# Two graph layers in fp32: half-width sums that share PSUM banks, mixes in a row, a reworked last pair and a new plan

## The chip, the cores and the metric

One core of a Trainium2 chip runs the kernel. The metric is the device time of one execution in microseconds; times are medians of the runs.

## What is computed

The input is x, 128 batches of 128 nodes with 512 features, and an adjacency matrix of 128 x 128 integers for each batch, all in fp32 or int32. Two layers follow each other, cut to what matters:

```python
# layer 0: attention with 8 heads of 64
q, k, v = (x @ W + b for W, b in ((Wq, bq), (Wk, bk), (Wv, bv)))
attn = softmax(where(adj > 0, q @ k.T / 8, -1e9))        # per head
x = layernorm(x + relu((attn @ v) @ Wo + bo))
# layer 1: graph attention
Wh = x @ W
e = leaky_relu((Wh @ a1)[:, None] + (Wh @ a2)[None, :], 0.2)
att = softmax(where(adj == 0, -1e9, e))
x = layernorm(x + elu(att @ Wh))
```

## The kernel before

Two batches are a pair, and there are 64 pairs. The two batches' rows make a matrix of 256 x 512 whose product with a weight of 512 x 512 is done in blocks in Strassen's manner: seven products of half size (PRODUCTS, L414) are summed in three PSUM banks, A (products 0 and 2), B (1, 3, 5) and C (4, 6). DVE and ScalarE add and subtract what the banks hold at fixed points in the row. The sums of blocks that the products take as operands are made on GpSimd, which the profile calls POOL (left_sums, L422; results sx, so, sz).

Per pair the steps are:
- q and k together: full-width products (columns_product, L528; banks of 128 x 512, 8 matmuls of 128 x 128 each). q^T and k^T come out, with biases added on ScalarE (with_bias, L614).
- v, o and w: half-width products (rows_product, L519; 2 matmuls of 128 x 256 each). Reading the banks takes half_p1, half_p6, half_c11, half_p7, half_c22, half_c21 and half_c12 (L709 to L774), which leave e1a, e1b, u2, u3 and the four blocks of the result (cv, co, cw).
- logits (L776): 8 matmuls per batch that use half of the rows of TensorE, into the pool ps_att. Masking, maximum, exponential, sum and scaling follow on DVE and ScalarE (L794 to L816).
- The weights of the softmax are transposed: by blocks of 32 on DVE, then through DRAM with a DMA out and four in (weights_t, weights_out, weights_in, L818 to L849). The last pair uses TensorE (ppT).
- mix_values (L851): 8 matmuls per batch that use half of the columns of TensorE, into po. mix_values_out (L860) adds bv on ScalarE and makes o^T (oT), the operand of the o products.
- residual, layer norm (L556 to L573; the steps rstd and shift on GpSimd), and the two edge sums per node on DVE (edge_term, L881).
- The edges of layer 1 (L891 to L960): the sums e_j are brought from a column into a row by a 32-wise transpose on DVE (ej) and four DMAs (ejr), e is summed on ScalarE, made leaky, masked and searched for its maximum on DVE, and raised on ScalarE (at). at is transposed by DVE and DMAs through DRAM (atb, atd, attT), but in the last pair on TensorE (pat, copied by ScalarE).
- mix_nodes (L962): 4 matmuls per batch into pz, copied to zT by ScalarE (L969), then the w products, elu (exponential on ScalarE, L991, the cut at one on GpSimd, L996, the maximum on DVE, L1000), residual and layer norm, and the store.

In the last pair side_engine (L418) puts GpSimd's sums and residuals on DVE, and the o and w products are plain ones with rows of the weights loaded again (plain_product, L690).

PSUM has these users: ps_att with two buffers of two banks (tag att), ps_acc with one bank for each of accA, accB and accC, and ps with one bank (tag ps), which po, pz, pat and the prologue's transposes share. With one buffer, the next user of a tag waits until the last reader of the one before is done.

The order of the work is written by hand. Each step is an event with a time of its own, and every engine, SyncE's DMA queue among them, takes its instructions in that order:

```python
shift = ENDS.get(p if p < n_pair // 2 else p - n_pair, {}).get(key, 0.0)
events.append((p * PERIOD + PLAN[key] + shift, len(events), fn, args))
```

The times are in the plan's own unit; only their order counts. A pair takes 36.74 us in the trace, between the starts of two logits. ENDS moves the steps of the first and last pairs, GOING (L284) puts unneeded matmuls (keep_going) behind some of them, and BUFS (L286) says how many buffers each SBUF tile has. The weights and biases are loaded by the lines L448 to L469: Wq, Wk and the first x on the queues of SyncE and ScalarE, Wv, Wo, W and a on SyncE's, the biases on GpSimd's.

Of the kernel before, what the change touches and what calls it, by code (L numbers as in the profile page):

```python
# [8 lines left out]
F32 = mybir.dt.float32  # L9
I32 = mybir.dt.int32  # L10
AF = mybir.ActivationFunctionType
# [6 lines left out]
PERIOD = 78.768558  # L18
PLAN = dict(
    load_adj=-214.2762, load_blocks=-156.4567, x_transpose0=-118.9579, sums_qk=-118.4185, sums_v=-116.8612,  # L20
    sums_fold1=-64.8766, x_transpose1=-64.055, sums_fold0=-58.8898, sums_fold_t1=-54.4418, qk0=-36.0224,
    x_sums=-35.8404, sums_fold_out1=-33.087, qk1=-32.9779, qk_p1=-31.7105, fill_logits0=-31.5232, qk4=-28.6459,
    qk_p6=-28.5331, sums_fold_t0=-28.2956, qk_p1q=-27.7049, qk2=-26.3155, qk_c11=-24.8916, sums_fold_out0=-23.0845,
    qk3=-22.6254, v0=-21.402, qk_p7=-19.9439, qk_c22=-19.9339, qk5=-14.7467, qk6=-13.4439, sums_o=-9.6234,
    qk_c21=-7.8856, qk_c12=-7.8498, v_p1=-4.7268, v1=-4.5449, fill_logits1=-1.8505, mask=-1.2435, v_p6=-0.2943,
    logits=0.0, mask_logits0=1.9952, max_logits0=3.7429, v3=4.4065, v_p7=4.433, v2=7.4467, v_c11=9.2069, v4=9.2085,
    mask_logits1=10.0374, load_x1=10.3213, v5=13.2871, v_c22=14.6665, exp_logits0=14.7511, v_c21=15.0921,
    v6=17.2266, v_c12=17.5754, max_logits1=22.1216, sum_logits0=24.0633, norm_logits0=27.409, exp_logits1=33.3029,
    weights_t0=43.7048, sum_logits1=43.7767, norm_logits1=52.0118, weights_out0=53.6197, weights_t1=55.6065,
    sums_w=66.7876, weights_out1=68.011, weights_in0=70.4393, weights_in1=74.301, mix_values0=75.8522,  # L30
    mix_values_out0=80.7212, mix_values1=81.4334, mix_values_out1=85.4398, load_x0=87.1711, o_sums=101.6394,
    o0=106.2181, o_p1=113.6365, o1=113.6652, o4=115.875, o_p6=116.2192, o_p1l=117.1503, o3=117.1603, o_p7=117.3205,
    o2=117.7709, o_c11=118.2449, o_c22=118.2872, o5=120.8539, o6=121.6955, o_c21=121.8792, residual01=122.7569,
    o_c12=122.7614, stats01=122.8191, mean01=123.8502, residual00=127.7304, rstd01=128.2803, shift01=128.7729,
    stats00=130.3078, norm01=131.2371, mean00=131.4538, rstd00=133.9815, edge_term01=134.3884, shift00=135.5918,
    edge_term11=137.3863, norm00=140.4496, edge_term10=144.2793, edge_blocks=146.1519, fill_edges=152.9599,
    edge_row=155.4786, edge_term00=159.9559, edge_sums=163.3873, edge_leaky=169.0665, edge_mask=174.9959,
    edge_max=179.2956, edge_exp=184.846, edges_t=185.9311, edges_t_out=188.282, edges_t_in=189.7663,
    mix_nodes1=211.95, mix_nodes_out1=218.2462, mix_nodes0=220.5122, mix_nodes_out0=222.7905, z_sums=231.0565,
    w0=248.2279, edge_norm=250.3865, w_p1=253.8429, w1=254.0225, w2=254.7456, w_p6=256.7486, w3=258.7144,  # L40
    w_c11=259.1252, w4=262.9461, w_p7=264.5461, w5=268.1992, w_c22=268.2862, w6=268.4953, w_c21=269.0061,
    w_c12=270.9016, elu_exp1=288.3615, elu_exp0=298.9658, elu_low1=307.1177, elu_max1=314.1197, elu_low0=326.1878,
    elu_max0=338.6625, residual10=340.2052, stats10=349.6362, mean10=349.9591, residual11=350.8328, rstd10=358.934,
    stats11=386.2458, mean11=395.8811, shift10=413.3316, rstd11=414.603, shift11=416.7025, finish0=436.5642,
    finish1=440.8676, store0=451.5942, store1=492.1186, tail_exp=492.2186, tail_max=492.3186, tail_sum=492.4186,
    tail_norm=492.5186)
# [3 lines left out]
        qk_p1=-683.1417, qk_p1q=-681.9305, x_transpose0=-638.4435, x_transpose1=-631.2847, qk_p6=-590.8687,  # L50
        load_adj=-509.98, qk0=-477.8452, qk1=-452.442, qk2=-417.202, qk_c11=-405.3261, load_blocks=-378.6558,
        qk_c21=-372.1296, load_x1=-349.2729, mask=-346.6978, fill_logits0=-342.4208, qk3=-323.1482,
        tail_max=-298.4256, qk_p7=-287.7433, load_x0=-275.5939, x_sums=-254.831, qk_c12=-246.448, logits=-211.8037,
        qk_c22=-200.6414, qk5=-195.7663, fill_edges=-195.5757, fill_logits1=-146.0062, mask_logits0=-117.0145,
        norm_logits0=-112.6679, v2=-110.5345, sum_logits0=-110.267, weights_t0=-109.2774, max_logits0=-108.9309,
        v_p1=-107.9734, mask_logits1=-107.2963, exp_logits0=-105.8888, sum_logits1=-105.473, exp_logits1=-105.4285,
        v4=-104.5453, v6=-103.1904, v3=-103.169, v_c22=-102.5766, v1=-102.4315, v_p6=-101.2639, v_c11=-99.6798,
        v5=-98.0298, weights_in0=-97.1349, weights_out0=-96.6864, norm_logits1=-96.608, weights_t1=-95.7185,
        max_logits1=-95.6542, v_p7=-94.2704, v0=-92.9615, v_c12=-91.0601, o_sums=-86.6133, v_c21=-85.4889,
        o0=-84.7601, o1=-84.5751, mix_values0=-83.3707, o_p6=-81.6679, o_p1=-81.5774, o4=-79.0618, o3=-76.7214,  # L60
        o_p1l=-75.7272, mix_values_out1=-73.9311, mix_values_out0=-73.1278, o_p7=-70.8784, mix_values1=-70.4988,
        edge_norm=-69.258, weights_in1=-63.5621, o2=-61.8681, o5=-61.4743, o_c11=-59.3031, weights_out1=-59.1716,
        qk6=-53.9952, o_c22=-52.8877, residual01=-49.6326, o6=-49.6072, o_c21=-49.0819, residual00=-47.774,
        o_c12=-45.863, rstd01=-45.0658, residual11=-44.5158, store1=-42.4846, mean01=-42.4551, stats01=-42.0697,
        stats11=-41.2343, shift01=-37.2547, edge_term00=-30.8626, stats00=-30.155, mean00=-28.7366, rstd00=-27.6003,
        edge_term10=-26.5946, norm00=-25.0273, elu_exp0=-23.9225, shift00=-21.9905, norm01=-20.8832,
        elu_low0=-20.7084, mean11=-19.7227, w4=-16.199, edge_term01=-15.574, elu_low1=-15.5655,
        edge_blocks=-13.5721, elu_max1=-12.3739, edge_term11=-11.5908, rstd11=-10.9852, edge_max=-9.6908,
        edge_exp=-8.7377, elu_exp1=-8.6133, w1=-8.084, mix_nodes_out1=-7.3656, w_c22=-6.8246, w_p7=-5.7838,
        edge_mask=-5.5201, w5=-5.2206, w_p6=-4.9532, w_c12=-4.7308, w3=-4.5677, w_c21=-4.3597, edge_leaky=-4.2136,  # L70
        w_p1=-3.3698, finish1=-3.265, w6=-2.9974, mix_nodes1=-2.7204, w2=-2.7129, w0=-2.5504, elu_max0=-2.5273,
        w_c11=-1.1757, edges_t=-0.4981, edge_sums=-0.4753, mix_nodes0=3.5821, edge_row=5.2807, z_sums=7.0497,
        edges_t_out=7.4547, mix_nodes_out0=8.0879, shift11=9.5854, residual10=10.3581, edges_t_in=10.9727,
        finish0=20.2363, shift10=23.2537, stats10=23.7054, store0=34.1326, tail_sum=34.4037, mean10=40.9196,
        rstd10=58.9908, tail_norm=87.4954, qk4=98.1821, tail_exp=109.5699),
    1: dict(
        tail_norm=-486.5775, tail_max=-214.9271, fill_logits1=-130.5901, qk0=-114.6075, qk2=-113.2598,
        qk_p1q=-111.8967, qk1=-111.4589, qk_p6=-110.7816, qk3=-109.5867, qk_p1=-109.3704, x_sums=-109.3159,
        qk_p7=-108.414, tail_sum=-106.3184, qk4=-104.0469, qk_c11=-94.7644, x_transpose1=-89.4256, v3=-88.8756,
        v0=-88.5843, v_p6=-88.4612, qk5=-86.7206, load_x0=-86.6125, v_p1=-86.0976, qk_c21=-85.9776, v1=-85.847,  # L80
        qk_c12=-83.5311, qk6=-80.4324, max_logits1=-78.9744, v5=-78.6397, qk_c22=-76.8719, v_c21=-75.782,
        v_c11=-75.0503, sum_logits0=-74.7479, v_c22=-74.6319, v2=-74.4777, v4=-73.6934, mask=-72.5388,
        mask_logits1=-72.5341, mask_logits0=-70.3835, v_p7=-70.2904, max_logits0=-69.0883, logits=-68.7397,
        exp_logits0=-68.0694, v6=-67.8706, v_c12=-66.1552, weights_t0=-62.7498, fill_logits0=-61.6049,
        x_transpose0=-60.9054, exp_logits1=-56.6504, sum_logits1=-54.1366, weights_out0=-53.2933,
# [199 lines left out]

BUFS = dict(  # L286
    at=1, xb=2, adj=5, so=1, xT=3, sx=1, pr=2, qT=2, kT=2, scr=1, cw=6, e1a256=1, mask=2, u2256=1, u3256=1, cv=2,
    x=3, prb=1, e1a512=1, e1b512=1, u2512=1, u3512=1, prT=2, oT=2, e1b256=1, co=6, ejr=1, e=1, atb=1, attT=1, zT=2,
    sz=1, t=2)


# [845 lines left out]
```

## Time and profile before

| | us |
|---|---|
| median of 3 runs | 2398.43 |
| lowest, highest | 2397.58, 2399.31 |
| profiled execution, its time | 2399.47 |
| its span, first to last instruction | 2397.7 |
| busy: TensorE matmuls | 2374.3 |
| busy: DVE | 1865.7 |
| busy: ScalarE | 1555.9 |
| busy: GpSimd | 1409.3 |
| mean granted TensorE clock | 0.998 |

The span is that of one execution taken by the hardware profiler, and it is 1.8 us shorter than that execution's time. PE is TensorE's matmuls, PEld its weight loads, which run beside them, DVE VectorE, ACT ScalarE, POOL GpSimd and SP SyncE. A line such as L525 is the line of the kernel that issued the instruction. An fp32 matmul is two instructions in the trace. The ends of matmuls are modelled, so the distance between two starts says more than a length. A wait in brackets is idle time of the engine before the instruction and what ended it.

### The profile page before, as it was taken

The page shows a single profiled execution, that of the slowest core. Times are in us where ns is not written, and L with a number is a line of the kernel's source. Part 1 is how long each engine was busy: PE and PEld are TensorE (multiplying, and loading weights), DVE is VectorE, ACT ScalarE, POOL GpSimd, SP SyncE. Part 2 cuts the span into 40 slices and gives each one's busy share as a digit, 9 for nine tenths or more (in the row PEclk, how much of TensorE's full clock was granted, in tenths as well). Part 3 has the DMA queues.
Part 4 walks back from the last instruction along what each step waited for, and adds up shares of the span by engine and source line. Part 5 has one row for each costly group of instructions (what it writes and reads, how often), then busy time and mean ns, then how long its engine had stood idle before and what let it go on. Part 6 is the DMA issues. An engine that isn't in the chain of part 4 may idle for free.

```text
span 2397.7 us, 51833 instructions
## 1 busy us (share of the span) xinstructions
PE 2374.3 (99%) x17750; PEld 2146.1 (90%) x17750; DVE 1865.7 (78%) x3883; ACT 1555.9 (65%) x5512; POOL 1409.3 (59%) x1988
## 2 busy tenths in 40 slices
PE   8999999999999999999999999999999999999997
PEld 8999999989989989899899899998998998989985
DVE  6777787787777777877877778778777777777786
ACT  4666676666666766766666667666666676666664
POOL 3455665656565656556665655565656565656557
PEclk9999999999999999999999999999999999999999
DMA  7534434444445344444444443544544534444433
GB/s 189 125 92 108 120 106 124 118 112 123 115 103 134 101 116 123 105 124 116 102 134 108 111 125 101 124 117 112 122 114 105 134 100 118 121 107 122 102 93 84
DMA packets 341366, 276.59 MB, mean 115 GB/s; under 512 B 126384, under 2 KB 288944, under 8 KB 341104
## 3 DMA queue, kind: packets, MB, share of 16 engines
q1 hardware_dynamic: 339712, 271.70, 44.2%
q8 instruction: 142, 2.33, 0.4%
q10 hardware_dynamic: 1216, 1.31, 0.3%
q14 instruction: 120, 0.98, 0.2%
q0 software_dynamic: 176, 0.27, 0.1%
HBM read 156.90 MB, written 107.87 MB: 110 GB/s over the span
## 4 chain that ended last, share of the span: by engine, by line
PE 95%; DMA 1%; POOL 1%; ACT 1%; DVE 1%; issue 0%; SPq 0%; ACTq 0%; POOLq 0%; DVEq 0%
PE pBqk L536 14%; PE pCqk L536 9%; PE pAqk L536 9%; PE pBv L525 7%; PE pBw L525 7%; PE pBo L525 7%; PE po L857 5%; PE s L784 5%; PE pz L967 5%; PE pAv L525 5%; PE pCv L525 5%; PE pAo L525 4%; PE pCo L525 4%; PE pAw L525 4%; PE pCw L525 4%; DMA wqk<-in_L_gnn_Wq_dram 0%
## 5 line engine op out<-in xcount | busy, mean ns | idle before, releaser
L807 ACT ACTIVATE pr<-pr,nmax 128x128 f32<-128x128 f32 x1024 | 395.2, 389 | 0.5 <-DVE nmax L801 0.5
L816 ACT ACTIVATE pr<-pr,tot 128x128 f32<-128x128 f32 x1024 | 314.4, 411 | 43.7 <-DVE tot L811 43.6
L866 ACT ACTIVATE oT<-po,bv 128x128 f32<-128x128 f32 x512 | 144.7, 364 | 290.4 <-PE po L857 290.4
L1009 POOL TENSOR_TENSOR cw<-cw,co 128x512 f32<-128x512 f32 x126 | 158.6, 1278 | 214.8 <-DVE cw L1003 214.8
L563 POOL TENSOR_SCALAR rstd<-mv 128x1 f32<-128x1 f32 x255 | 95.2, 373 | 271.1 <-DVE mv L558 250.1
L998 POOL TENSOR_SCALAR t<-t 128x512 f32<-128x512 f32 x126 | 246.3, 1955 | 9.0 <-ACT t L994 8.6
L536 PE MATMUL pAqk<-xT,wqk 128*128 128x128 f32 x2016 | 245.7, 275 | 2.2 <-ACT e1bqk L616 2.2
L536 PE MATMUL pBqk<-sx,wqk 128*128 128x128 f32 x2016 | 245.6, 275 | 0.4 <-POOL rstd L563 0.4
L536 PE MATMUL pCqk<-sx,wqk 128*128 128x128 f32 x2016 | 245.7, 275 | 0.0
L536 PEld LDWEIGHTS pAqk<-xT,wqk 128*128 128x128 f32 x2016 | 236.4, 192 | 9.3 <-ACT e1bqk L616 2.4
L536 PEld LDWEIGHTS pBqk<-sx,wqk 128*128 128x128 f32 x2016 | 239.8, 192 | 3.8 <-POOL rstd L563 0.5
L536 PEld LDWEIGHTS pCqk<-sx,wqk 128*128 128x128 f32 x2016 | 235.5, 192 | 0.2
L792 POOL MEMSET pr<- 128x1024 f32 x128 | 121.8, 951 | 145.2 <-DVE prb L826 145.2
L888 DVE SCALAR_TENSOR_TENSOR scr<-co,wa_bc 128x512 f32<-128x512 f32 x256 | 185.4, 724 | 16.9 <-ACT co L573 11.6
L796 DVE COPY_PREDICATED pr<-mask,s 128x1024 f32<-128x1024 int32 x128 | 171.6, 1341 | 33.5 <-PE s L784 33.3
L807 ACT ACTIVATION_READ_ACCUMULATOR pr<-pr,nmax 128x1 f32 x1024 | 193.6, 189 | 0.0
L826 DVE STREAM_TRANSPOSE prb<-pr 128x1024 f32<-128x1024 f32 x126 | 156.1, 1239 | 17.6 <-ACT pr L816 16.5
L564 POOL TENSOR_TENSOR rstd<-rstd,half 128x1 f32<-128x1 f32 x255 | 145.5, 571 | 21.2
L801 DVE TENSOR_REDUCE nmax<-pr 128x8 f32<-128x1024 f32 x128 | 155.4, 1214 | 0.2
L857 PE MATMUL po<-prT,cv 128*64 128x128 f32 x2048 | 140.0, 279 | 0.1
L967 PE MATMUL pz<-attT,co 128*128 128x128 f32 x1024 | 136.8, 277 | 2.6 <-DMA attT<-atd 1.3
L525 PE MATMUL pBv<-wv,sx 128*128 128x256 f32 x512 | 137.4, 391 | 0.0
(197 smaller groups left out, 5920.0 us busy)
## 6 DMA issues: line engine op xcount, KB each, us to landing
prd<-prb SPq DMA_DIRECT2D x126, 512.0 KB, 2.9
prT<-prd SPq DMA_DIRECT2D x504, 128.0 KB, 3.6
x<-in_x_dram SPq DMA_DIRECT2D x128, 256.0 KB, 4.4
out_dram<-cw SPq DMA_DIRECT2D x128, 256.0 KB, 3.5
xb<-in_x_dram SPq DMA_DIRECT2D x252, 128.0 KB, 4.0
adj<-in_adj_dram SPq DMA_DIRECT2D x64, 128.0 KB, 2.1
ejr<-ej SPq DMA_DIRECT2D x256, 32.0 KB, 3.9
atd<-atb SPq DMA_DIRECT2D x63, 128.0 KB, 1.8
```

The lines of the kernel that those rows point to most:

```text
L525: nc.tensor.matmul(out, left_block(left, blk.pair, a_i, c), right_block(weight, b_i)[:, c, :], start=first and c == 0, stop=j in LAST and ...
L536: nc.tensor.matmul(out[:, f * P:(f + 1) * P], weight[:, b_i, c, f * P:(f + 1) * P], left_block(left, blk.pair, a_i, c), start=first and f ...
L796: nc.vector.copy_predicated(PR[b], MASK[p][:, i, :].unsqueeze(1).to_broadcast([P, H, P]), ST.pop(("s", b)).rearrange("p j h k -> p (j h) k"))
L801: nc.vector.tensor_reduce(NMAX[b], PR[b], AX.X, ALU.max, negate=True)
L807: nc.scalar.activation(PR[b][:, h, :], PR[b][:, h, :], AF.Exp, bias=nmax[:, h:h + 1], scale=1.0, accum_out=TOT[b][:, h:h + 1])
L816: nc.scalar.activation(PR[b][:, h, :], PR[b][:, h, :], AF.Copy, scale=tot[:, h:h + 1])
L826: nc.vector.transpose(PRB[b].rearrange("p k h s -> p h k s"), PR.pop(b).rearrange("p h (k r) -> p h k r", r=32))
L857: nc.tensor.matmul(ST["o", b][j * DH:(j + 1) * DH, hp, :], v[:, h * DH:(h + 1) * DH], prT[:, :, j * (H // 2) + hp, :], start=True, stop=True)
L888: nc.vector.scalar_tensor_tensor(scr, X1[b], 1.0, wa_bc[s], op0=ALU.mult, op1=ALU.mult, accum_out=acc)
L967: nc.tensor.matmul(ST["z", b][:, c, :], X1[b][:, c * P:(c + 1) * P], attT, start=True, stop=True)
L998: side_engine(b // 2).tensor_scalar(t, t, 1.0, -1.0, op0=ALU.min, op1=ALU.add)
L1009: side_engine(b // 2).tensor_tensor(Y[b], Y[b], X1.pop(b), op=ALU.add)
```

## The change

Six things are changed together:
- Blocks.psum: half-width sums A and C lie side by side in one bank, in accA for v and w and in accC for o. B stays in accB. Full-width sums keep three banks. In the last pair the plain o product A goes to accC.
- mix_values of the odd batch writes to accC instead of ps, so that the two mixes need not take turns. In the order, most pairs ran a mix, the logits of the next pair, and the other mix; now they run the logits and then both mixes.
- For the last pair: half of the scaling of the softmax goes to DVE, half of the reads of po and pz too, and the row of e_j is made by two DVE copies and two transposes on TensorE into PSUM, from where e is summed, in place of a DVE transpose and four DMAs.
- at is transposed on TensorE in the last two pairs, not in the last alone.
- bo is loaded by SyncE's queue behind a, not by GpSimd's.
- PERIOD, PLAN, ENDS, GOING and BUFS are new. In the first pair the plain q and k products run A, B, C, D, A, B, C, D instead of A, B, A, B, C, D, C, D.

The diff, with the tables PLAN and ENDS left out:

```diff
-PERIOD = 78.768558
+PERIOD = 81.828156
...
-GOING = {('w6', -3): 5, ('mix_nodes1', -2): 2, ('mix_nodes0', -2): 2, ('w2', -2): 2, ('w5', -2): 4, ('edges_t', -1): 1, ('mix_nodes1', -1): 2}
+GOING = {('edges_t', -2): 2, ('mix_nodes1', -2): 3, ('mix_nodes0', -2): 3, ('w0', -2): 2, ('edge_row', -1): 1, ('w6', -2): 5, ('edges_t', -1): 2, ('mix_nodes1', -1): 4}
...
-    at=1, xb=2, adj=5, so=1, xT=3, sx=1, pr=2, qT=2, kT=2, scr=1, cw=6, e1a256=1, mask=2, u2256=1, u3256=1, cv=2,
-    x=3, prb=1, e1a512=1, e1b512=1, u2512=1, u3512=1, prT=2, oT=2, e1b256=1, co=6, ejr=1, e=1, atb=1, attT=1, zT=2,
+    at=1, xb=2, adj=3, so=1, xT=4, sx=1, qT=2, kT=2, pr=2, e1a256=2, u2256=1, mask=1, cv=2, u3256=1, scr=1, cw=6,
+    prb=1, e1a512=1, e1b512=1, u2512=1, u3512=1, prT=2, oT=2, x=2, e1b256=2, co=6, ejr=1, e=1, atb=2, attT=1, zT=2,
     sz=1, t=2)
...
-    nc.gpsimd.dma_start(bo_bc, bass.AP(tensor=bo.tensor, offset=bo.offset, ap=[[0, P], [1, D]]))
+    nc.sync.dma_start(bo_bc, bass.AP(tensor=bo.tensor, offset=bo.offset, ap=[[0, P], [1, D]]))
...
         def psum(self, bank):
             if bank not in self.bank:
-                self.bank[bank] = ps_acc.tile([P, self.width], F32, tag=f"acc{bank}", name=f"p{bank}{self.tag}_{self.name}")
+                if self.width == D or bank == "B":
+                    self.bank[bank] = ps_acc.tile([P, self.width], F32, tag=f"acc{bank}",
+                                                  name=f"p{bank}{self.tag}_{self.name}")
+                else:
+                    t = ps_acc.tile([P, D], F32, tag="accC" if self.tag == "o" else "accA",
+                                    name=f"pAC{self.tag}_{self.name}")
+                    self.bank["A"], self.bank["C"] = t[:, 0:HALF], t[:, HALF:D]
             return self.bank[bank]
...
-            b.bank[bank] = ps_acc.tile([P, D], F32, tag=f"acc{bank}", name=f"p{bank}{tag}_last")
+            b.bank[bank] = ps_acc.tile([P, D], F32, tag="accC" if tag + bank == "oA" else f"acc{bank}",
+                                       name=f"p{bank}{tag}_last")
...
     def norm_logits(b):
         tot = TOT.pop(b)
-        for h in range(H):
+        shared = H // 2 if b // 2 == n_pair - 1 else H
+        for h in range(shared):
             nc.scalar.activation(PR[b][:, h, :], PR[b][:, h, :], AF.Copy, scale=tot[:, h:h + 1])
+        if shared < H:
+            nc.vector.tensor_tensor(PR[b][:, shared:H, :], PR[b][:, shared:H, :],
+                                    tot[:, shared:H].unsqueeze(2).to_broadcast([P, H - shared, P]), op=ALU.mult)
...
-        ST["o", b] = ps.tile([P, H // 2, P], F32, tag="ps", name=f"po_{b}")
+        pool, tag = (ps_acc, "accC") if b % 2 else (ps, "ps")
+        ST["o", b] = pool.tile([P, H // 2, P], F32, tag=tag, name=f"po_{b}")
...
         for f in range(NC):
-            nc.scalar.activation(OT[b][:, f, :], po[:, f, :], AF.Identity, bias=bv_sb[:, f:f + 1], scale=1.0)
+            if p == n_pair - 1 and f % 2:
+                nc.vector.tensor_scalar(OT[b][:, f, :], po[:, f, :], bv_sb[:, f:f + 1], None, op0=ALU.add)
+            else:
+                nc.scalar.activation(OT[b][:, f, :], po[:, f, :], AF.Identity, bias=bv_sb[:, f:f + 1], scale=1.0)
...
     def edge_blocks(p):
 
+        if p == n_pair - 1:
+            rows = buf([P, 2, P], F32, "ejr", f"ejr_{p}")
+            for i in range(2):
+                nc.vector.tensor_copy(rows[:, i, :], ej_blocks[p % 3][:, 32 * i:32 * i + 1].to_broadcast([P, P]))
+            ST["j", p] = rows
+            return
...
     def edge_row(p):
 
+        if p == n_pair - 1:
+            rows = ST["j", p]
+            ST["j", p] = ps.tile([P, 2, P], F32, tag="ps", name=f"pj_{p}")
+            for i in range(2):
+                nc.tensor.transpose(ST["j", p][:, i, :], rows[:, i, :], ident)
+            return
...
         for i in range(2):
-            nc.scalar.activation(e[:, i, :].rearrange("p (v s) -> p v s", s=32), j[:, :, 32 * i:32 * i + 32],
-                                 AF.Identity, bias=ei[:, i:i + 1], scale=1.0)
+            if p == n_pair - 1:
+                nc.scalar.activation(e[:, i, :], j[:, i, :], AF.Identity, bias=ei[:, i:i + 1], scale=1.0)
...
     def edges_t(p):
 
-        if p < n_pair - 1:
+        if p < n_pair - 2:
...
     def edges_t_out(p):
-        if p < n_pair - 1:
+        if p < n_pair - 2:
...
         ATT[p] = buf([P, 2, P], F32, "attT", f"attT_{p}")
-        if p < n_pair - 1:
+        if p < n_pair - 2:
...
-        nc.scalar.copy(ZT[b], ST.pop(("z", b)))
+        z = ST.pop(("z", b))
+        if p == n_pair - 1:
+            nc.scalar.copy(ZT[b][:, 0:2, :], z[:, 0:2, :])
+            nc.vector.tensor_copy(ZT[b][:, 2:4, :], z[:, 2:4, :])
+        else:
+            nc.scalar.copy(ZT[b], z)
```

## The prediction

> **What bounds the kernel.** I read the page first (busy shares, then the chain that ended last), then the busy times by stretch of the span, then TensorE's timeline in a steady pair and the last 60 us.
>
> ```profile
> PE 2374.3 (99%) x17750; PEld 2146.1 (90%) x17750; DVE 1865.7 (78%) x3883; ACT 1555.9 (65%) x5512; POOL 1409.3 (59%) x1988
> ...
> PE 95%; DMA 1%; POOL 1%; ACT 1%; DVE 1%; issue 0%; SPq 0%; ACTq 0%; POOLq 0%; DVEq 0%
> ```
>
> TensorE is busy 99% and makes 95% of the chain. Columns of the next view: stretch, its length, busy time (instructions) of PE, PEld, DVE, ACT and POOL, clock, DMA share, GB/s.
>
> ```profile
> 200.00:2300.00 2100.00, 2099.60 (x15756) 1903.37 (x15756) 1644.96 (x3433) 1384.70 (x4916) 1253.75 (x1766) 1.00 0.45 115
> ...
> 2340.00:2398.00 58.00, 42.34 (x214) 31.00 (x214) 38.50 (x84) 24.89 (x54) 42.63 (x60) 0.92 0.31 85
> ```
>
> In the middle TensorE lacks 0.4 us of 2100, so only cheaper or fewer matmuls can shorten it. The last 58 us lack 15.7 us, and POOL is busier there than TensorE. "Busy" hides one cost: the time that a matmul takes beyond its kind's usual pace. It shows in start-to-start times:
>
> ```profile
> 622.59 1.95 PE L536 MATMUL pCqk<-sx,wqk 128*128 128x128 f32 x16
> 624.37 1.03 PE L525 MATMUL pBv<-wv,sx 128*128 128x256 f32 x4
> 625.33 1.09 PE L857 MATMUL po<-prT,cv 128*64 128x128 f32 x16
> 626.36 2.06 PE L784 MATMUL s<-kT,qT 64*128 64x128 f32 x32
> 628.34 1.09 PE L857 MATMUL po<-prT,cv 128*64 128x128 f32 x16
> 629.37 1.13 PE L525 MATMUL pBv<-wv,sx 128*128 128x256 f32 x4
> 630.33 1.03 PE L525 MATMUL pAv<-wv,xT 128*128 128x256 f32 x4
> ```
>
> Columns: start, length, engine, line, operation; x counts instructions, two for each fp32 matmul. A half-width product undisturbed takes 0.864 us (598.78 to 599.64 below), a full-width one 1.786 (16 instructions), so a mix (po, 16) should take 0.893 and the logits (s, 32) 1.786. Here pBv before po takes 0.96 (+0.10), po to s 1.03 (+0.13), s to po 1.98 (+0.20), po to pBv 1.03 (+0.13), the pBv behind it 0.96 (+0.10). The trace marks the three kinds 128*128, 64*128 and 128*64; each change of kind costs 0.1 to 0.2 us, 0.66 us in a pair. Check: a pair's undisturbed work is 7 full products 12.50, 21 half-width 18.14, logits 1.79, two mixes 1.79, two pz 1.79, together 36.01; with 0.66 and 0.08 (next view) that is 36.75, and the chain has logits start every 36.74 us.
>
> ```profile
> 598.78 1.03 PE L525 MATMUL pAw<-w,zT 128*128 128x256 f32 x4
> ...
> 599.04 0.42 DVE L732 TENSOR_TENSOR u2w<-pBw,e1aw 128x256 f32<-128x256 f32 x1 [0.50 <-PE pBw L525]
> ...
> 599.64 1.06 PE L525 MATMUL pBw<-w,sz 128*128 128x256 f32 x4
> ...
> 600.54 1.03 PE L525 MATMUL pCw<-w,sz 128*128 128x256 f32 x4
> ```
>
> This is a cover of one product. pBw must wait until u2w has read the bank; pAw alone lies between. u2w ends at 599.46, and pBw then takes 0.90 in place of 0.864: the cover just misses, by 0.04, twice a pair. DVE was free when the data came; that is the condition.
>
> **The change, part by part.** *Order of logits and mixes.* By the instruction order, 59 pairs ran mix, logits, mix; now 63 run logits, mix, mix, the odd mix in bank accC. Changes of kind fall from 262 to 193. In a steady pair the switch po to s (0.13) goes; product to s stays near the 0.10 of product to po; the rest remains: -0.13 us. Over 60 pairs -8 us; by 69 fewer switches of 0.10 to 0.20 it is -7 to -14. I take -8, the pair's own rows. The Trainium skill speaks against any gain: "TensorE: Matmul & The Clock Gate", Measured speedup vs the span model, puts the cost of a further tile at about 4 ns and has no term for a change of tiling, which gives 0 for this edit; "TensorEngine Tiling (Array Packing)", Tiling Modes, Key Properties, says that changing the mode drains the array, without a price. The rows side with the second and price it; I use them.
>
> *Shared banks.* v and w put A and C into the halves of accA, o into accC. Where C once had its own bank, its first product now waits on TensorE for the read of A (c11), and the next user of the bank for c22 and c12; TensorE works in order, so all its later products wait with it. In the order about nine half-width reads per pair have one product of cover (u2, u3, c11 and c22 of w among them), against two seen to miss by 0.04. Queued ahead of them on DVE are 1.34 us masks (L796), 1.21 us maxima (L801) and 0.72 us edge sums (L888); ScalarE's c11 stands behind 0.39 us exponentials. Below: no more misses than now, 0.08; above: nine of 0.04, 0.36. From walking the new order I take three to four, 0.12: +0.04 a pair, +2.5 us in all. Steady sum: -5.5 us (-8 to +9). The second mix no longer has the logits ahead of it as cover for its weights' DMA: 3 us less. By the order its loads (3.6 us median landing) are issued early enough; I take nothing.
>
> *Buffers.* adj, mask and x lose spare copies, xT, e1a, e1b and atb gain one. By the plan x is read 16 of a period's 82 units, 7 us, or more after its load is issued, which takes 4.4 us; adj's loads take 2.1. Zero while that holds, and if a load came late, its residual would wait on DVE with every eviction behind it.
>
> *bo.* Its 256 KB leave POOL's queue, where nothing of the start stands behind them, and go behind a_bc on SP's, ahead of the x and adj loads there; its first use was at 60.7 us. In the first 40 us DMA moves about 245 GB/s, so the early loads gain at most 1 us. The start's products are also reordered A, B, C, D, A, B, C, D, so Wk is wanted 3.6 us sooner, and TensorE already lacks 6.5 us in those 40. From -1.5 to +2; I take 0.
>
> *The end.* The rows, before:
>
> ```profile
> 2361.31 1.13 PE L967 MATMUL pz<-attT,co 128*128 128x128 f32 x8 [1.26 <-DMA attT<-atd]
> ...
> 2365.57 3.25 SPq L901 DMA_DIRECT2D ejr<-ej  x4
> ...
> 2372.40 0.69 ACT L911 ACTIVATE e<-ejr,ei 128x128 f32<-128x128 f32 x2 [2.24 <-DVE cw L1003]
> ...
> 2377.01 0.71 PE L944 MATMUL pat<-ident,at 128*128 128x128 f32 x2 [2.42 <-ACT at L929]
> 2377.56 0.39 PE L1051 MATMUL keep_going<-ident 128*128 128x128 f32 x2
> 2378.04 3.81 POOL L998 TENSOR_SCALAR t<-t 128x512 f32<-128x512 f32 x2 [2.37 <-ACT t L994]
> 2378.26 2.08 PE L967 MATMUL pz<-attT,co 128*128 128x128 f32 x8 [0.31 <-ACT attT L960]
> ```
>
> Pair 62 loses one write and four reads of attT by DMA (2.6 us of the chain) for two transposes (0.7 as pat) and a ScalarE copy (0.35): pz can start 1.5 us earlier, since 1.3 us of fillers and 1.26 of idleness stand before it. Pair 63's edge row took 7.1 us from ej (2365.30) to e (2372.40), four DMA issues in it; now two DVE copies (about 0.3 each by the 0.28 of a 128x256 DVE row), two transposes (0.7), straight into e: 1.3 us, 5.8 less. The steps from e to pat (4.6 us) stay. w's last evictions of pair 62 (c12 at 2376.35) stand behind these edges on DVE and come earlier with them, and so does the elu of pair 62 on POOL (2378.04), from which the chain runs to the end with POOL nearly full. So about 5 us pass to the end. pz at 2378.26 took 2.08 for 0.89 after the 2.42 us wait, at a lower granted clock (0.92 in this stretch); with four more fillers some of that 1.2 stays away: 1 more. Splitting the last softmax scaling, mix and z reads between ScalarE and DVE removes 8 x 0.41 + 4 x 0.36 + 0.4 from ScalarE, but TensorE is busy with other products until 2358.8: 0 to -1, I take 0. Below: only 1.5 if POOL holds its place; above: of TensorE's 30.6 us from 2358.8 to its last matmul, 6.1 are waits, some 4.5 fillers and 1.2 slow clock, so -11. I take -6.
>
> Sum against the profiled execution: 2399.5 (span 2397.7 and 1.8 around it) - 5.5 - 6 = 2388. The median of the three runs, 2398.4, lies 1.0 below that execution: **2387**.
>
> **Rivals.**
> - *Both gains, in the sizes above*: 2381 to 2391. For it: the priced switches; the idle 15.7 us. Chance 0.54.
> - *More covers miss*: 0.1 us a pair more, +6: 2390 to 2395. For: nine covers with no slack to speak of. Against: a miss is 0.04 and DVE is 22% idle. Chance 0.20.
> - *All of it and more* (69 switches at full price, clock kept): 2375 to 2381. Chance 0.05.
> - *The change doesn't do what it says*: reads of the shared banks eat the switches, and the end stays tied to POOL (42.6 of 58 us busy), whose steps the change leaves as they are: 2398, 2394 to 2403. Chance 0.12.
> - *Slower*: one read with one product of cover stands in every pair behind a 1.34 us mask or a 1.21 us maximum on DVE. DVE then starts it up to 1.3 us late, and the rest of the cover lost stalls TensorE 0.5 us: 60 x 0.5 = +30 against -14: 2414; with half of it 2399 to 2405. It is slower than 2403 from (14 + 4.8) / 60 = 0.31 us a pair on. Against: in the rows above DVE had waited 0.50 us when its data came, and the new plan, too, can leave DVE free there. Chance 0.09.
>
> **How the numbers follow.** A measurement of this kernel tells about 0.2% (4.8 us) from no change. Faster (under 2393.6): 0.54 + 0.05 + 0.20 of the second case's larger part, 0.79. Same: 0.13. Slower: 0.08. The range 2378 to 2395.5 takes the first case, nearly all of the second and half of the third; some 0.2 is left out.
>
> **What would show it.** Right: logits start every 36.63 to 36.68 us, with po twice in a row behind s; no po ahead of the logits; the end's last logits-to-end stretch (80.4 us) shortened to 74 to 76; pat of pair 63 near 2371 less the steady gain; pz after it at 0.9 us. Wrong: half-width products of 1.0 us or more at fixed places in each pair, with TensorE's rows naming u2, u3, c11 or c22; a logits spacing of 36.74 or more; POOL's elu at the same distance from the end as before.

## The result, and the profile after

The changed kernel takes 2388.72 us (median of 6 runs, 2388.07 to 2389.04), the kernel before 2397.82 in runs beside it: a ratio of 0.9961, 95% interval 0.9948 to 0.9973, or 9.1 us faster. The forecast was 2387 (2378 to 2395.5). The profiled execution took 2388.57 us, its span is 2386.6. Busy shares and the chain that ended last, from the page of after:

```profile
PE 2365.3 (99%) x17762; PEld 2148.1 (90%) x17762; DVE 1903.9 (80%) x3891; ACT 1539.4 (65%) x5501; POOL 1401.3 (59%) x1987
...
PE 96%; ACT 1%; DVE 1%; DMA 1%; POOL 1%; issue 0%; SPq 0%; POOLq 0%; ACTq 0%; DVEq 0%
```

TensorE runs 12 more instructions and is busy 9 us less: the gain is inside its busy time. TensorE's timeline in a steady pair of after, the answer to the seven lines of before:

```profile
1062.56 1.03 PE L532 MATMUL pBv<-wv,sx 128*128 128x256 f32 x4
1063.42 1.03 PE L532 MATMUL pACv<-wv,xT 128*128 128x256 f32 x4
1064.38 2.06 PE L792 MATMUL s<-kT,qT 64*128 64x128 f32 x32
1066.37 1.97 PE L870 MATMUL po<-prT,cv 128*64 128x128 f32 x32
1068.26 1.13 PE L532 MATMUL pBv<-wv,sx 128*128 128x256 f32 x4
1069.23 1.03 PE L532 MATMUL pACv<-wv,sx 128*128 128x256 f32 x4
```

By start-to-start times the product ahead of s takes 0.96 (+0.10), s 1.99 (+0.20), the two mixes together 1.89 (+0.10 on 1.786), the product behind them 0.97 (+0.10). That is 0.51 us of switches for 0.66. Logits of steady pairs now start every 36.58 us; before it was 36.73 to 36.74.

The sum by stretch, in two profiles of the kernel before (the one on record, and one of a repeated run whose execution took 2395.26 us), and one of after:

| start of logits, us | before | before, again | after |
|---|---|---|---|
| pair 0 | 23.51 | 23.30 | 25.36 |
| pair 6 | 222.35 | 222.17 | 222.52 |
| last pair (63) | 2317.29 | 2316.86 | 2308.21 |
| from pair 6 to the last | 2094.94 | 2094.69 | 2085.69 |
| from the last to the end | 80.4 | 76.6 | 78.4 |

The 9.1 us lie between pair 6 and the last pair. Of these, 0.8 us is work that has only moved out of the stretch: by its instructions it holds two half-width products of v less than before (1.73 us) and one mix more (0.89). What is saved there is 8.2 to 8.4 us. The start is neutral: logits 0 are 2 us later because two of v's products (1.8 us) now run ahead of them, and by pair 6 the difference is 0.2 to 0.4 us. The end is, on balance, no shorter than before: the first profile of before had a long one. It now holds one of v's products more (0.86 us).

### The profile page after: what moved, and what is told of

It reads as the page before. It is cut to its first block, busy times and chain, and to the rows that moved or that the text cites. A ratio compares the mean times of both kernels' runs of the same rounds, so it can differ in the third digit from the quotient of the medians.

```text
span 2386.6 us, 51852 instructions
## 1 busy us (share of the span) xinstructions
PE 2365.3 (99%) x17762; PEld 2148.1 (90%) x17762; DVE 1903.9 (80%) x3891; ACT 1539.4 (65%) x5501; POOL 1401.3 (59%) x1987
## 4 chain that ended last, share of the span: by engine, by line
PE 96%; ACT 1%; DVE 1%; DMA 1%; POOL 1%; issue 0%; SPq 0%; POOLq 0%; ACTq 0%; DVEq 0%
PE pBqk L543 14%; PE pAqk L543 9%; PE pCqk L543 9%; PE pACo L532 9%; PE pACv L532 9%; PE pACw L532 9%; PE pBv L532 7%; PE pBo L532 7%; PE pBw L532 7%; PE s L792 5%; PE po L870 5%; PE pz L998 5%; ACT pr L815 0%; DMA xb<-in_x_dram 0%; ACT pr L825 0%
## 5 line engine op out<-in xcount | busy, mean ns | idle before, releaser
L430 POOL TENSOR_TENSOR so<-oT 128x256 f32<-128x256 f32 x63 | 45.9, 729 | 392.4 <-ACT oT L882 392.4
L1034 POOL TENSOR_SCALAR t<-t 128x512 f32<-128x512 f32 x126 | 243.9, 1948 | 26.3 <-ACT t L1030 25.9
L904 DVE SCALAR_TENSOR_TENSOR scr<-co,wa_bc 128x512 f32<-128x512 f32 x256 | 219.3, 857 | 2.7 <-ACT co L580 2.4
L815 ACT ACTIVATION_READ_ACCUMULATOR pr<-pr,nmax 128x1 f32 x1024 | 215.6, 211 | 0.0
L933 POOL MEMSET at<- 128x256 f32 x64 | 19.9, 311 | 304.1 <-DVE atb L971 304.1
L657 DVE TENSOR_TENSOR u3qk<-pBqk,e1aqk 128x512 f32<-128x512 f32 x63 | 43.5, 690 | 149.2 <-PE pBqk L543 149.1
L792 PEld LDWEIGHTS s<-kT,qT 64*128 64x128 f32 x2048 | 119.3, 188 | 20.8 <-DVE kT L678 17.6
```

Source lines behind the costliest of these rows:

```text
L792: nc.tensor.matmul(ST["s", b][:, j, hp, :], q[r, hp, :], k[r, hp, :], start=True, stop=True)
L815: nc.scalar.activation(PR[b][:, h, :], PR[b][:, h, :], AF.Exp, bias=nmax[:, h:h + 1], scale=1.0, accum_out=TOT[b][:, h:h + 1])
L904: nc.vector.scalar_tensor_tensor(scr, X1[b], 1.0, wa_bc[s], op0=ALU.mult, op1=ALU.mult, accum_out=acc)
L1034: side_engine(b // 2).tensor_scalar(t, t, 1.0, -1.0, op0=ALU.min, op1=ALU.add)
```

## Experiments

Each experiment ran beside the kernel before on one chip. Differences of a few us in the end are smaller than the intervals of the ratios, so the end is read in the traces, from the start of the last logits: five profiles whose last pair is that of after, unchanged but for fillers or bo, gave 78.25 to 78.52 us.

### The steady pair

**e1_mix_split**, of the changed kernel:

```diff
-    weights_in0=76.8757, mix_values0=83.0319, weights_in1=83.7749, mix_values1=84.6403, mix_values_out0=86.1105,
+    weights_in0=76.8757, mix_values0=81.7, weights_in1=83.7749, mix_values1=84.6403, mix_values_out0=86.1105,
```

> The changed kernel with one edit of its plan: the even mix stands ahead of the logits again, the odd one behind them; shared banks, buffers and the last pair as changed. Theory (the steady gain is the switch that went): the switch from a mix to the logits, 0.13 to 0.15 us, comes back in each pair; logits every 36.71 to 36.73 us in place of 36.58, 8 to 9.5 us slower than the changed kernel in all, 2396.7 to 2398.2. Rival (the gain is in the covers and buffers of the new plan, not in the order): under 2 us slower.

Measured: 2437.07 us, 1.0155 of before (1.014 to 1.017); logits every 37.44 us, 0.86 more than after (medians). The first two lines, in TensorE's timeline, show the switch back; the rest is a second price. DVE and TensorE, a steady pair:

```profile
1085.74 1.09 PE L870 MATMUL po<-prT,cv 128*64 128x128 f32 x16
1086.77 2.06 PE L792 MATMUL s<-kT,qT 64*128 64x128 f32 x32
...
1089.99 1.22 DVE L809 TENSOR_REDUCE nmax<-pr 128x8 f32<-128x1024 f32 x1
...
1091.73 0.43 DVE L762 TENSOR_TENSOR u3v<-pBv,e1av 128x256 f32<-128x256 f32 x1
1092.21 1.13 PE L532 MATMUL pBv<-wv,xT 128*128 128x256 f32 x4 [0.44 <-DVE u3v L762]
```

po takes 1.03 again, 0.13 over its pace; with the 0.02 that the two mixes lose by being apart, that is the theory's 0.15. The other 0.71: only one mix now lies between the logits and v's next product, DVE still has the mask and the maximum of these logits and two edge sums in hand, and u3v comes too late for its single covering product: pBv starts 0.61 us late and takes 0.10 more. So the theory had the switch right and took the covers for unaffected; its total of 8 to 9.5 us was far too small. Logits and both mixes in a row also buy DVE a product's time.

**e2_before_row**, of the kernel before, pairs 6 to 57:

```diff
+        if key == "mix_values0" and 6 <= p < n_pair - 6:
+            shift += 3.05
...
-        ST["o", b] = ps.tile([P, H // 2, P], F32, tag="ps", name=f"po_{b}")
+        pool, tag = (ps_acc, "accC") if b % 2 and 6 <= b // 2 < n_pair - 6 else (ps, "ps")
+        ST["o", b] = pool.tile([P, H // 2, P], F32, tag=tag, name=f"po_{b}")
```

> The kernel before with one edit, in pairs 6 to 57: the even mix behind the logits, the odd one in bank accC; no shared banks, no new plan. Theory (the order alone carries the steady gain, the shared banks only make room): 52 pairs save 0.15 us where no wait comes in, 36.58 us between logits, -8 us, 2390. Rival (without the shared halves the third bank is wanted by v's C product while ScalarE still reads the second mix from it): TensorE waits for oT ahead of pCv, 0.2 to 1 us a pair, which takes the gain and makes it equal to before or up to 40 us slower.

Measured: 2407.51 us, 1.0034 (1.0023 to 1.0045), logits 36.90 us apart in the edited pairs. The rival holds. ScalarE and TensorE behind the mixes:

```profile
1076.85 1.15 ACT L867 ACTIVATE oT<-po,bv 128x128 f32<-128x128 f32 x4
1076.97 1.03 PE L525 MATMUL pAv<-wv,xT 128*128 128x256 f32 x4
...
1078.05 1.13 PE L525 MATMUL pCv<-wv,sx 128*128 128x256 f32 x4
1079.02 1.03 PE L525 MATMUL pAw<-w,zT 128*128 128x256 f32 x4
```

pCv needs accC and starts when oT has been read from it (1078.00): 1.08 us after pAv, 0.22 late, and then takes 0.97. The row of mixes saves 0.15 and this wait costs 0.32. The shared halves are what leaves accC free for the second mix.

**e3_late_max**, of the changed kernel:

```diff
+        if key == "max_logits1" and 6 <= p < n_pair - 6:
+            shift += 14.0
```

> The changed kernel with one DVE instruction of each of the pairs 6 to 57 moved: the maximum of the odd batch's logits (1.21 us) stands right ahead of u3w, a read with one product of cover. Theory of the slow rival (a long instruction ahead of a covered read stalls TensorE by what it sticks out): u3w starts 0.5 to 1.2 us late, pBw waits as long; 52 x 0.5 to 52 x 1.2, 26 to 62 us slower than the changed kernel. Rival (the slack ahead of u3w, and the cover, take it): under 5 us slower.

Measured: 2433.83 us, 1.0141 (1.0121 to 1.0162), 45 us more than after. DVE and TensorE:

```profile
1095.26 1.21 DVE L809 TENSOR_REDUCE nmax<-pr 128x8 f32<-128x1024 f32 x1
1096.39 0.41 DVE L762 TENSOR_TENSOR u3w<-pBw,e1aw 128x256 f32<-128x256 f32 x1
...
1096.86 1.13 PE L532 MATMUL pBw<-w,zT 128*128 128x256 f32 x4 [0.66 <-DVE u3w L762]
```

One step of 1.2 us at the wrong place in DVE's order costs 0.82 us per pair on the product's start and 0.10 on its length, and a later product loses its miss of 0.04; 52 times 0.88 are 46 us. The prediction's slow rival was a real danger, at a higher price than it set. In the changed kernel, by its own timeline below, u2w ended at 1075.09 and the next pBw started at 1075.27, 0.86 after the product ahead:

```profile
1074.41 1.03 PE L532 MATMUL pACw<-w,zT 128*128 128x256 f32 x4
1074.67 0.42 DVE L740 TENSOR_TENSOR u2w<-pBw,e1aw 128x256 f32<-128x256 f32 x1 [0.77 <-ACT e1aw L727]
...
1075.27 1.07 PE L532 MATMUL pBw<-w,sz 128*128 128x256 f32 x4
1076.18 1.03 PE L532 MATMUL pACw<-w,sz 128*128 128x256 f32 x4
```

The miss shows in the pBw (0.91 for 0.864). It comes twice a pair, as before. In a steady pair of after, ten reads end 0.18 to 0.33 us before the start of the product that needs their bank; three of them end at 0.18, and only two of those three products take 0.04 us longer. The other eight run at their pace.

### The end and the start

**e11_bo_pool**, bo back on GpSimd's queue:

```diff
-    nc.sync.dma_start(bo_bc, bass.AP(tensor=bo.tensor, offset=bo.offset, ap=[[0, P], [1, D]]))
+    nc.gpsimd.dma_start(bo_bc, bass.AP(tensor=bo.tensor, offset=bo.offset, ap=[[0, P], [1, D]]))
```

> The changed kernel with bo loaded by GpSimd's queue as before. Theory of the prediction (256 KB at 245 GB/s are 1 us of the loads that TensorE waits for at the start): the Wk block lands up to 1 us later and the first logits start 0 to 1 us later, most of it made good by later waits: 0 to 1 us slower. Rival (bo delays nothing that is waited for): within 0.3 us.

Measured: 2390.14 us, 0.9970 (0.9958 to 0.9981); logits 0 at 25.91, pair 6 at 223.05. The changed kernel and the nine others of these experiments with its start had logits 0 anywhere from 24.54 to 25.88. If bo costs the start anything there, it is of the size of this scatter; whether it does stays open.

**e5_t62_dma**: in edges_t, edges_t_out and edges_t_in

```diff
-        if p < n_pair - 2:
+        if p < n_pair - 1:
```

and the write of pair 62 moved right behind DVE's transpose.

> The changed kernel with the attention weights of layer 1 of pair 62 transposed as before, by DVE and through DRAM, the write issued as soon as DVE is done. Theory (before, pz of pair 62 waited 1.26 us for these DMAs behind 1.28 us of fillers; in the changed kernel it starts with no wait): pz of pair 62 starts 1.5 to 2.5 us later, and since the sums for pair 62's w products and the edges of pair 63 follow it on POOL and DVE, the end comes 1 to 2 us later. Rival (the wait of DVE for pair 63's norm hides it): within 0.5 us.

Measured: 2391.82 us, 0.9975 (0.9965 to 0.9985); from the last logits to the end 81.95, 3.5 more than after. TensorE:

```profile
2355.33 1.92 PE L998 MATMUL pz<-attT,co 128*128 128x128 f32 x8 [3.30 <-DMA attT<-atd]
```

pz starts 47.23 us behind the last logits instead of 44.28, and is 1.92 us long where after has 1.16. The delay passes to the end in full; I had expected 1 to 2. This is what the transposes on TensorE are worth in the new order.

**e4_edges_dma**: in edge_blocks, edge_row and edge_sums

```diff
-        if p == n_pair - 1:
+        if p == n_pair:
```

> The changed kernel with the last pair's row of e_j made as before, by a DVE transpose and four DMAs, and e summed from SBUF. Theory (behind the row, the sums ei of the same pair are next late: in the changed kernel e starts at 2363.15, 3.1 us after the row is there): only what the DMAs exceed this by is lost; they land some 6.5 us after ej, near 2365, e starts 2 us later, and the end comes 1 to 2 us later. Rival (the row's round trip is worth what it took before): e and the end come 5 to 6 us later.

Measured: 2389.72 us, 0.9959 (0.9944 to 0.9974); e starts 56.55 us behind the last logits (after: 54.94), the end is 80.7 behind (78.4). The theory holds in the main: 1.6 us of the 5.8 that the prediction had taken off the row are felt at e, because ei was next late. The end's 2.3 us are a little above the 1 to 2.

**e6_act_only**: in norm_logits, mix_values_out and mix_nodes_out

```diff
-        shared = H // 2 if b // 2 == n_pair - 1 else H
+        shared = H
...
-            if p == n_pair - 1 and f % 2:
+            if False:
...
-        if p == n_pair - 1:
+        if False:
             nc.scalar.copy(ZT[b][:, 0:2, :], z[:, 0:2, :])
```

> The changed kernel with the last pair's scaling, po reads and z reads on ScalarE alone. Theory of the prediction (TensorE has other work while the softmax of the last pair runs): 0 to 1 us slower. Rival (in the changed order po of the last pair already waits for ScalarE, 0.7 and 1.4 us in the trace, so 3.3 us more on ScalarE before po and 0.7 after it are felt): 2 to 4 us slower.

Measured: 2389.87 us, 0.9968 (0.9956 to 0.9980); the end 79.2 us behind the last logits, 0.8 more than after. The prediction's bound holds.

**e10_no_fillers**: no unneeded matmuls at the end (the 22 from GOING).

```diff
-            events.append((p * PERIOD + PLAN[key] + shift, len(events), keep_going_late, (GOING[key, p - n_pair],)))
+            pass
```

> The changed kernel without the 22 unneeded matmuls at its end. They fill 4.9 us of TensorE's time there. Theory (they keep the granted clock up through the waits): without them TensorE idles longer, pz and the last products run at a lower clock, 1 to 4 us slower. Rival (no effect on the clock, or they stand in the way): 0 to 1 us faster.

Measured: 2389.78 us, 0.9970 (0.9960 to 0.9981); the end 78.3 us behind the last logits. In this program they neither help nor hurt. Without them TensorE waits up to 1.79 us at a time, and its granted clock (the third figure from the right) stays at 1.00. In the kernel before, pz of pair 63, behind pat's wait of 2.42 us, ran at 0.50. The stretch of e10 first, then that pz of before:

```profile
2352.00:2372.00 20.00, 13.25 (x68) 9.69 (x67) 15.51 (x34) 8.51 (x19) 17.41 (x22) 1.00 0.17 54
...
2378.26:2380.40 2.14, 2.14 (x10) 2.14 (x11) 0.48 (x2) 1.30 (x3) 2.14 (x2) 0.50 0.29 111
```

What is late instead of the row? These are the rows of after that lead to pair 63's edges:

```profile
2357.18 1.15 DVE L904 SCALAR_TENSOR_TENSOR scr<-co,wa_bc 128x512 f32<-128x512 f32 x1 [1.59 <-ACT co L580]
...
2359.56 2.93 POOL L1045 TENSOR_TENSOR cw<-cw,co 128x512 f32<-128x512 f32 x2
2359.61 1.76 DVE L904 SCALAR_TENSOR_TENSOR scr<-co,wa_bc 128x512 f32<-128x512 f32 x1
2359.63 0.44 PE L924 MATMUL pj<-ident,ejr 128*128 128x128 f32 x2
...
2361.64 1.41 DVE L904 SCALAR_TENSOR_TENSOR scr<-co,wa_bc 128x512 f32<-128x512 f32 x1
...
2363.15 0.62 ACT L940 ACTIVATE e<-pj,ei 128x128 f32<-128x128 f32 x2 [3.76 <-DVE scr L904]
...
2366.98 0.56 PE L975 MATMUL pat<-ident,at 128*128 128x128 f32 x2
```

The row is in PSUM at 2360.1, but e waits until 2363.15 for the last edge sum. Three of the four sums took 1.15, 1.76 and 1.41 us, the first 0.65; in both profiles of before three of them took 0.67 to 0.69 and one 0.87 or 0.88. POOL adds pair 61's residuals during the last two, and makes sz during the 1.15. **e7_resid61_dve** takes that work away from POOL:

```diff
-            side_engine(b // 2).tensor_tensor(Y[b], Y[b], X1.pop(b), op=ALU.add)
+            eng = nc.vector if b // 2 in (n_pair - 3,) else side_engine(b // 2)
+            eng.tensor_tensor(Y[b], Y[b], X1.pop(b), op=ALU.add)
```

with their events, statistics and means put behind w_c12 of pair 62.

> The changed kernel with the two residual sums of pair 61 taken from POOL, where they ran 2.9 us at 2359.6 beside pair 63's edge terms, and put on DVE behind the last read of pair 62's w. Theory (the edge terms ei, the last to be ready for pair 63's edges, took 1.76 and 1.41 us for 0.69 because POOL works at the same time): both take 0.7 to 0.9, e starts 1.3 to 1.8 us earlier, and the end comes 0.5 to 1.5 us earlier. Rival (DVE is slow there for another reason, or the added 1.4 us on DVE are felt): e at the same distance from the last logits, the end 0 to 1.5 us later.

Measured: 2390.66 us, 0.9971 (0.9959 to 0.9982). In its timeline:

```profile
2358.63 0.68 DVE L904 SCALAR_TENSOR_TENSOR scr<-co,wa_bc 128x512 f32<-128x512 f32 x1
...
2359.57 0.67 DVE L904 SCALAR_TENSOR_TENSOR scr<-co,wa_bc 128x512 f32<-128x512 f32 x1
...
2370.53 1.81 PE L998 MATMUL pz<-attT,co 128*128 128x128 f32 x8 [3.02 <-DVE zT L1006]
```

The cause is shown: with POOL's sums gone the two take 0.68 and 0.67, and e starts 2.05 us sooner behind the last logits (52.89). The gain is not passed on, though, and the end is 2.2 us later (80.7): the half read of zT on DVE stands behind elu_max of pair 62, which waits for POOL's cut, and TensorE waits 3 us with it. **e8_elu62_dve**, of the changed kernel, puts pair 62's cuts (L1034) and residuals on DVE, in elu_low and residual1 alike:

```diff
-        side_engine(b // 2).tensor_scalar(t, t, 1.0, -1.0, op0=ALU.min, op1=ALU.add)
+        eng = nc.vector if b // 2 == n_pair - 2 else side_engine(b // 2)
+        eng.tensor_scalar(t, t, 1.0, -1.0, op0=ALU.min, op1=ALU.add)
```

> The changed kernel with pair 62's elu cut and residual on DVE instead of POOL. In the changed kernel the chain of the end runs through these POOL steps: 3.85 us for the cuts and 2.5 for the residuals, on DVE 2 x 0.43 and 2 x 0.69. Theory (POOL sets the end, the prediction's rival): 1 to 3 us faster. Rival (TensorE's last product and the steps behind it set the end; POOL's steps lie beside them): within 0.5 us.

Measured: 2388.11 us, 0.9960 (0.9947 to 0.9972); the end 77.9 us behind the last logits, 0.5 less than after. The gain of 1 to 3 did not come: these POOL steps do not set the end. **e9_both** makes both edits, the residuals with:

```diff
+            eng = nc.vector if b // 2 in (n_pair - 3, n_pair - 2,) else side_engine(b // 2)
```

> The changed kernel with pair 61's residuals and pair 62's elu cuts and residuals on DVE, the two edits before this one together. Theory (POOL both slows DVE and holds the end): the gains add, 2 to 4 us faster than the changed kernel. Rival (TensorE's products and the last steps behind them set the end): under 1 us faster.

Measured: 2388.26 us, 0.9963 (0.9951 to 0.9976); the end 77.4 us behind the last logits, 1.0 less than after, with the same time within the interval. So most of the time that the edge sums lose beside POOL does not reach the end. No version beat the changed kernel by more than its runs scatter.

**before_again**, the kernel before without an edit.

> The kernel before once more, for a second profile: the profile on record was of an execution 1.7 us above the median. Logits 36.73 us apart as before; a difference from the first profile can lie in the start, in single longer pairs (37.08 us twice), or in the end. If it lies in the end, the end's gain by the change is smaller than the two first profiles say.

Measured: 2398.24 us (1.0003, 0.9995 to 1.0012); this profile is of the first of its runs, at 2395.26. The difference to the profile on record lies in the end:

```profile
2359.08 1.06 PE L967 MATMUL pz<-attT,co 128*128 128x128 f32 x8
...
2373.49 0.71 PE L944 MATMUL pat<-ident,at 128*128 128x128 f32 x2 [1.15 <-ACT at L929]
...
2374.74 1.16 PE L967 MATMUL pz<-attT,co 128*128 128x128 f32 x8 [0.31 <-ACT attT L960]
```

Here SyncE issued the reads of attT 1.7 us sooner (2355.53 for 2357.21; from the last logits 1.25), pz of pair 62 did not wait, pair 63's pat waited 1.15 us for 2.42, and its pz ran at the usual pace. The end took 76.6 us for 80.4; e2_before_row, whose end is that of before, took 78.0.

The 1.25 us are not the DMAs' own. One step ahead of them, DVE's masking of pair 62's edges, took 0.45 us here and 1.53 in the profile on record. Here first, then the profile on record:

```profile
2351.33 0.45 DVE L919 COPY_PREDICATED at<-adj,e 128x256 f32<-128x256 int32 x1
2351.68 1.27 POOL L1009 TENSOR_TENSOR cw<-cw,co 128x512 f32<-128x512 f32 x1
...
2351.89 1.27 POOL L1009 TENSOR_TENSOR cw<-cw,co 128x512 f32<-128x512 f32 x1
2351.94 1.53 DVE L919 COPY_PREDICATED at<-adj,e 128x256 f32<-128x256 int32 x1
```

Where DVE started first, neither was slowed. Where POOL was 0.05 us ahead, DVE's step ended 0.30 us after POOL's sum. That is 1.08 of the 1.25 us; how the rest of the 3.8 us arises behind it was not tested.

## Why the prediction was right, point by point

- **Switches: right, a little small.** The rows' 0.13 us a pair was 0.15, since two mixes in a row also end with 0.11 instead of 0.13. Over 57 pairs that is 8.6 us, where I took 8. A model with no term for such a change would have given 0; e1 and the timeline show the price.
- **Covers of the shared banks: mis-sized.** I took 0.12 us a pair for the misses; they cost 0.09, against 0.08 before. I had let three to four reads miss; two do. This term of the sum, +2.5 us, measured +0.6, and with the switches that is -8.0 where I had -5.5. The table's stretch gives 8.2 to 8.4.
- **Slow rival: a real mechanism that did not occur.** e3 and e1 show 0.9 and 0.7 us a pair when a long step stands ahead of such a read; I had put 0.5.
- **The end: the step that failed.** I took -6. From the last logits it measured 78.4 us, where three profiles with the end of before have 80.4, 76.6 and 78.0 (mean 78.3). Less the v product that moved into it, the gain is 2.8 us against the profile that I had, and about 0.8 against the mean. I also measured from a long end; a step of DVE that POOL held up makes part of its length. The three parts are worth about what I took, 3.5 (attT of pair 62), 2.3 (edge row) and 0.8 (split reads), each measured against its own undoing in the new order. What failed is that I left the work around them where it was, so that each part would bring the end forward by its own size. The new order gives it back ahead of them: the last matmul of the last pair's o product starts 43.0 us behind the last logits, before 39.8 to 40.2. Of these 2.8 to 3.2 us, 1.7 are two half-width products that now stand ahead of it, the one of v and the last of pair 61's w; the rest, 1.1 to 1.5, is longer waiting of TensorE, the most of it for ScalarE's zT, 1.43 and 0.70 us in after for 0.76 and 0.20:

```profile
2334.08 1.16 PE L998 MATMUL pz<-attT,co 128*128 128x128 f32 x8 [1.43 <-ACT zT L1008]
...
2336.96 1.57 PE L870 MATMUL po<-prT,cv 128*64 128x128 f32 x16 [0.70 <-ACT zT L1008]
```

So pz of pair 62, which I had 1.5 us earlier, starts 44.3 us behind the last logits, before 42.2 to 44.0. For the row I took 5.8 us off e; e starts at 54.9, before 52.8 to 55.1, in part because the edge sums that it waits for take 2 us more beside POOL (e7). Freed of that, and of pair 62's steps on POOL, the end gains 1.0 (e9). The extra fillers, for which I took 1 us, are worth nothing (e10). What makes ScalarE's zT later, and how the rest divides among the new order's steps, stays open. pat of pair 63 came at 2366.98, where 2371 less the 9 us by which the last logits come earlier is 2362.
- **Start: right**, 0 was taken, and pair 6's logits are 0.2 to 0.4 us later, inside the scatter of 1.5 us that the changed start shows over its profiles.

So the total was right by luck: two errors of opposite sign, about 3 us on the steady part and about 5 on the end. The forecast of 2387 lay 1.7 us below 2388.72. In the chances, the 0.79 for faster counts the second case whole, though only the larger part of it lies under 2393.6.

## What to carry to other kernels

When one engine is busy all the time, look at how long its instructions take beyond their own pace; neighbours of another kind are a cost that busy time hides. A reordering that saves such a cost needs banks and free readers at the right moment, and is lost where a long instruction stands ahead of a read with a short cover. Take a stretch made of short waits from several executions before its gain is put into a sum. A saving counts only as far as the next input is ready, so ask what is next late.

## What the runs showed of the hardware

- DVE's edge sums, which read two operands from SBUF, took 1.15 to 1.76 us beside POOL's sums and 0.65 to 0.69 without them. The Trainium skill's "SBUF — State Buffer", section SBUF: two separate sides, says that such a DVE instruction and a GpSimd one that reads SBUF keep each other out for a whole instruction, and that the one that starts first goes first; the rows agree, and moving POOL's work away restored the time. Over the whole run these sums average 0.86 us in after and 0.72 in before; in a steady pair TensorE's rows show no cost of it.
- The same collision differs between executions of one program. DVE's masking took 1.53 us where POOL's sum had started 0.05 us before it, and 0.45 where DVE was first. That is 1.08 of the 1.25 us by which the DMAs behind it were issued later, measured from the last logits.
- A change between full tiles, half rows and half columns cost TensorE 0.09 to 0.23 us each in fp32, 0.66 us for mix, logits, mix and 0.51 for logits, mix, mix.
- TensorE's granted clock stayed at 1.00 through waits of up to 1.79 us (e10_no_fillers), and was 0.50 in the pz behind the wait of 2.42 us in before.
